# Routing in groups of 16 under a budget of time per step, and first tiles of the second pass prepared within the first

## The chip, the cores and the metric

One core of one Trainium2 chip runs one program. Its engines work side by side, each through its own queue: TensorE (PE, its weight loads shown as PEld), VectorE (DVE), ScalarE (ACT), GpSimd (POOL) and SyncE (SP). SP and POOL issue the DMAs here; POOL's are indirect ones (gathers and scatters by a list of rows). The metric is the device time of one execution in microseconds. The time before is 1279.0 us, the median of 8 runs (1277.34 to 1280.34).

## The reference

x has 16x1024 tokens of 512 numbers. What is computed, cut to what matters (`D` is a number that depends on all of the normalized x):

```python
def reference(x, W_el, b_el, W_le, b_le, router_w, expert_weights):
    xn = layernorm(x)                                   # per token
    # first branch: a filter, and a code word of 24 bits that is corrected
    D = fractal_dimension(xn)
    x1 = ifft(fft(xn) * wave_filter(D, 512)).real
    bits = (sigmoid(x1 @ W_el + b_el) > 0.5)            # 24 per token
    s = x1 + golay_correct(bits) @ W_le + b_le
    # second branch: 8 experts, the best two of each token
    logits = xn @ router_w.T
    probs = softmax(logits)
    topk_vals, topk_idx = top_k(probs, 2)
    topk_w = topk_vals / (topk_vals.sum(-1) + 1e-6)
    expert_out = einsum('nh,eho->eno', xn, expert_weights)
    g = silu(((take(expert_out, topk_idx) + topk_vals) * topk_w).sum())
    return x + s * g
```

## The kernel before

The 16384 tokens are 128 tiles of 128 (`NT`), and the program has two passes. In the first every tile of tokens is filtered, its code word and its two experts are found, and a record of each token (two weights, a bias, mean, scale, token number, corrected bits) is scattered into the list of its pair of experts (28 pairs). In the second pass tokens are gathered by pair, so that all 128 tokens of a tile use the same two expert matrices.

**Pass 1** is the loop of `pass_1` (L1107 to L1190) over g, one tile per step. SP loads x in blocks of four tiles (`load_block`, pool `xin` of 5 buffers, issued `AHEAD_L` = 16 steps ahead) and stores the filtered rows yd in blocks of four. For each tile: DVE folds the rows into sums and differences (`fold`, L445 and L448), ACT takes the sum of squares (`spread`, L459), PE transposes (`transpose`, L528 and L532) and ACT copies the result, PE multiplies by the filter matrix (`filt`, L542), ACT copies yb out (L548), and a step later DVE's `take` (L472) sums the last columns of the product: 8 logits, 24 latent values, and what the mean and scale need.

Around them run many small operations of DVE, kept in lists of closures. `scale` (L477) turns the raw sums of a group of `GT` = 8 tiles into mean and scale, `code` (L560) finds and corrects the bits of such a group, `route` (L631) works on 16 tiles (`RT`): the largest two logits, the pair, the softmax weights, and each token's place in its list, by products with a triangular matrix in PE, a product with a mask (`place`) and a sum (`where`, both of 128x448 numbers). One list each is popped at fixed points of a step: the order below is that of every step, whatever the operations cost.

```python
            routed()
            steps(scales, 1)
            routed()
            steps(now, 1)
            while folds and folds[0][0] <= g:
                fold(*folds.pop(0)[1:])
```

When a round's places are known, POOL scatters one tile's records with each DMA (`lists<-rec,dst`, L791), one or two per step (`throw`). After `SOON` = 80 tiles, `whole_ops` (L861 to L964) finds which full tiles of 128 each pair has by then: POOL gathers their records (`tt`, L915) once the scatters due have been issued, and DVE takes them apart (L926) five steps later. At g = NT-10, NT-4 and NT-1 the first tile of pass 2 is gathered (`lead_x`), normalized and turned. The last group's `scale` is run after the last step.

**Pass 2** (from L1195) has 189 tiles in the order that `kinds` writes out: 28 wholes (`LEAD`), 61 items (tiles of one expert, made of what is left over) mixed with 8 wholes, 5 wholes, and 27 rests (the left-over tokens, whose two products were stored by items) mixed with 60 wholes. I call the stretch of rests and wholes the tail. What is left of routing and the bookkeeping of lists runs within its first steps, and with it the remaining scatters (up to three per step).

Step n of the loop works on products of tile n and on other tiles' earlier and later parts. POOL's queue gets, in this order: `fetch_tok(n+11)` (for items, the entry's gather), `fetch_x(n+8)` (xg, L1082 by way of `gather`), `fetch_parts(n+4)` (two gathers for a rest), `fetch_y` (yg), and `put` of tile n-4 (out, L1433). xg takes a buffer of the pool `xgp` of 14; a tile's result is formed in that same buffer (L1424) and out reads it from there, while an item's buffer is free after `normalize`.

```python
    AHEAD_K, AHEAD_X, AHEAD_P, AHEAD_Y, AHEAD_N, AHEAD_T = 11, 8, 4, 5, 6, 3
    BEHIND = 3
    xgp = ctx.enter_context(tc.tile_pool(name="xgp", bufs=14))
```

DVE gets `normalize(n+6)` (L1267), `triple` (L1339 and L1340: the bits of a tile as b3, 4 steps ahead), `spread_out` and `combine` (L1371 to L1378, L1423, L1424: the first branch joined to the second), and `added` (L1384) or the item's copy (L1395). PE gets the products (L1324; two per whole, one per item, each 8 records), `turn` (L1276) for the first tiles, `turn_code` (L1354) and `mend` (L1366: corrected bits through W_le). ACT gets `scaled` (L1381) and the Silu (L1387), and the halves (L1283) and joins (L1292) around SP's DMA transposes, which replace `turn` from the seventh tile on.

Of the kernel before, what the change touches and what calls it, by code (L numbers as in the profile page):

```python
# [23 lines left out]
ENTRY = META  # L24
IN_RANGE = "worked out on the chip from counts that add up to the number of tokens"
# [9 lines left out]
def kernel(  # L35
# [57 lines left out]
    SOON = 80  # L93
# [24 lines left out]
    xin = p1.enter_context(tc.tile_pool(name="xin", bufs=5))  # L118
# [55 lines left out]
    def loads():  # L174
        nc.sync.dma_start(out=head, in_=xf[0:2, :].rearrange("t (a j) -> (t a) j", j=HW))
        nc.sync.dma_start(out=bas, in_=basis)
        for b in range(2):
            xts[b] = load_block(b, 2 - b)
        nc.scalar.dma_start(out=lat, in_=w_lat)
        nc.scalar.dma_start(out=ident, in_=square[:, 0, :])  # L180
        xts[2] = load_block(2)
        nc.sync.dma_start(out=ht, in_=golay_t)
        nc.sync.dma_start(
            out=row_sb,
            in_=rows.rearrange("(o n) -> o n", o=1).to_broadcast([P, rows.shape[0]]),
        )
        nc.sync.dma_start(out=tri, in_=square[:, 1, :])
        nc.sync.dma_start(out=wl, in_=w_le3)
        nc.sync.dma_start(out=ord_sb, in_=orders)
        for b in range(3, 5):  # L190
            xts[b] = load_block(b)
# [212 lines left out]
    GT = 2 * TPT  # L404
    NG = NT // GT
    AHEAD_L = 16
    RT = 2 * GT
    rounds = [(t, RT) for t in range(0, NT, RT)]

# [6 lines left out]
    recs = [p1c.tile([P, 2 * GT, META], F32, name=f"rec{i}") for i in range(4)]  # L416
# [10 lines left out]
    for s in range(NG):  # L427
        groups[s].rec = recs[(s // 2) % 4][:, (s % 2) * GT : (s % 2 + 1) * GT, :]
# [48 lines left out]
    def scale(s: int):  # L477
# [9 lines left out]
        def off():  # L487
            nc.gpsimd.tensor_copy(k.rec[:, :, MEAN], k.raw[:, :, X])
# [15 lines left out]
        def scaled():  # L504
            if s % 2 == 0:
                k.wide = small.tile([P, 2 * GT, X], F32, name="ex", bufs=2)
                k.ex = k.wide[:, 0:GT]
            else:
                k.ex = groups[s - 1].wide[:, GT:]
# [10 lines left out]
            scaled,  # L520
# [39 lines left out]
    def code(s: int):  # L560
# [64 lines left out]
        turns = [lambda: turn_bits(0), lambda: turn_bits(TPT)]  # L625
        checks = [c0, c1, c2, c3, c4, c5]
        return [bits] + [None] * 5 + turns + [None] * 4 + [syndrome] + [None] * 2 + checks
# [3 lines left out]
    def route(n: int):  # L631
# [6 lines left out]
        def new(name, shape, dt=F32):  # L638
            full = [P, {S: 2 * GT}.get(shape[1], shape[1])] + list(shape[2:])
            made = small.tile(full, dt, name=name, bufs=4 if name == "dst" else 1)  # L640
            return made[:, 0 : shape[1]]
# [7 lines left out]
        def begin():  # L649
            s, j = t0 // GT, t0 % GT  # L650
            st.ex = groups[s].wide[:, j : j + S]
            st.rec = recs[(t0 // (2 * GT)) % 4][:, t0 % (2 * GT) : t0 % (2 * GT) + S, :]
            st.mx = st.m1 = new("mx", [P, S])
            v.tensor_reduce(st.mx, st.ex[:, :, L:X], AX.X, ALU.max)
            v.tensor_copy(st.rec.bitcast(I32)[:, :, TOKEN], tok[:, t0 : t0 + S])

        def shift():
            st.pb = new("pb", SN)
            v.tensor_tensor(st.pb, st.ex[:, :, L:X], wide(st.mx), ALU.subtract)
            nc.scalar.activation(st.pb, st.pb, AF.Exp)  # L660

        def total():
            st.sm = new("sm", [P, S])
            st.den = new("den", [P, S])

            st.ch = small.tile([P, 2, S], F32, name="ch", bufs=1)
            st.wt = small.tile([P, 2, S], F32, name="wt2", bufs=1)
            v.tensor_reduce(st.sm, st.pb, AX.X, ALU.add)


        def largest(src, hot):
            def b():
                st.eq = new("eq", SN)
                v.tensor_tensor(st.eq, src(), wide(st.mx), ALU.is_equal)

            def d():
                st.at = new("at" + hot, [P, S])
                setattr(st, "at" + hot, st.at)
                v.tensor_reduce(st.at, st.eq, AX.X, ALU.max)

            def e():
                setattr(st, hot, new(hot, SN))
                v.tensor_tensor(getattr(st, hot), rv, wide(st.at), ALU.is_equal)

            return [b, lambda: v.tensor_mul(st.eq, st.eq, rv), d, e]

        def rest():
            st.pr = new("pr", SN)
            v.scalar_tensor_tensor(
                st.pr, st.hot1, -1e30, st.ex[:, :, L:X], ALU.mult, ALU.add  # L690
            )

        def second():
            st.mx = new("m", [P, S])
            v.tensor_reduce(st.mx, st.pr, AX.X, ALU.max)

        ops = [begin, shift]
        ops += largest(lambda: st.ex[:, :, L:X], "hot1")
        ops += [rest, second] + largest(lambda: st.pr, "hot2")

        def chosen():

            st.sel = new("sel", [P, S, NE + NE // 2], BF16)
            v.tensor_add(st.sel[:, :, 0:NE], st.hot1, st.hot2)
            v.tensor_copy(st.sel[:, :, NE:], st.sel[:, :, 0 : NE // 2])

        def behind():

            st.p2 = new("p2", [P, S])
            v.tensor_tensor(st.p2, st.mx, st.m1, ALU.subtract)  # L710
            nc.scalar.activation(st.p2, st.p2, AF.Exp)

        ops += [chosen, behind]
        chances = [
            total,
            lambda: v.reciprocal(st.ch[:, 0, :], st.sm),
            lambda: v.tensor_mul(st.ch[:, 1, :], st.p2, st.ch[:, 0, :]),
            lambda: v.scalar_tensor_tensor(  # L718
                st.den, st.ch[:, 0, :], 1e-6, st.ch[:, 1, :], ALU.add, ALU.add
            ),  # L720
            lambda: v.reciprocal(st.den, st.den),
        ]


        def pair(d, at):
            if d == 1:
                st.oh = new("oh", [P, S, NPAIR], BF16)
            n = min(NE, NPAIR - at)
# [4 lines left out]
        for d in range(1, NE // 2 + 1):  # L733
            ops.append(lambda d=d: pair(d, (d - 1) * NE))

        A = S // 4
# [42 lines left out]

        def place():  # L780
            st.pl = new("pl", [P, S, NPAIR])
            v.tensor_mul(st.pl, st.pk, st.oh)

        def where():
            st.dst = new("dst", [P, S], I32)
            with nc.allow_low_precision("whole numbers"):
                v.tensor_reduce(st.dst, st.pl, AX.X, ALU.add)
# [17 lines left out]
        def weigh():  # L805
            v.tensor_mul(st.wt, st.ch, st.den.unsqueeze(1).to_broadcast([P, 2, S]))

        def biases():

            v.tensor_mul(st.ch, st.ch, st.wt)  # L810

        def swap():

            st.lo = new("lo", [P, S])
            v.tensor_tensor(st.lo, st.athot1, st.athot2, ALU.is_gt)
            v.tensor_sub(st.den, st.wt[:, 0, :], st.wt[:, 1, :])

        weights = [
            weigh,
            biases,  # L820
            lambda: v.tensor_add(st.rec[:, :, BIAS], st.ch[:, 0, :], st.ch[:, 1, :]),
            swap,
            lambda: v.tensor_mul(st.lo, st.lo, st.den),
            lambda: v.tensor_add(st.rec[:, :, W0], st.wt[:, 1, :], st.lo),
            lambda: v.tensor_sub(st.rec[:, :, W1], st.wt[:, 0, :], st.lo),
        ]
        ranks = [None, place, where]
# [7 lines left out]
        ops += [quads, runs, None, rank] + chances + weights  # L835
# [244 lines left out]

    def gather(dst, src, idx, limit):
# [25 lines left out]
    def pass_1():  # L1107
        scales = []

        def steps(ops, n):  # L1110
            for _ in range(min(n, len(ops))):
                op = ops.pop(0)
                if op:
                    op()
# [15 lines left out]
        )  # L1130
        loaded = 0
        for g in range(-1, NT):
            if (g + AHEAD_L) % TPT == 0 and 5 <= (g + AHEAD_L) // TPT < NB:
# [14 lines left out]
            if g > 0 and g % GT == 0:  # L1148
                scales += scale(g // GT - 1) + [lambda s=g // GT - 1: now.extend(code(s))]
            for n, (t, size) in enumerate(rounds):  # L1150
                if g == t + size + 4:
                    routes.extend(route(n))
                    if t + size == SOON:
                        routes.append(lambda: whole_ops(0))
            going = True

            def routed():
                nonlocal going
                going = going and bool(routes) and routes[0] is not None
                if going:  # L1160
                    going = routes[0]() is not False
                if going:
                    routes.pop(0)

            routed()
            steps(scales, 1)
            routed()
            steps(now, 1)
            while folds and folds[0][0] <= g:
                fold(*folds.pop(0)[1:])  # L1170
                steps(rest, 1)
            steps(now, 1)
            routed()
            steps(scales, 1)
            routed()
            if going is False and routes and routes[0] is None:
                routes.pop(0)
            steps(now, 1)
            steps(rest, 1)
            if g < NT - TPT:  # L1180
                throw(1 + (g > SOON))
            push(aside)
            if g == NT - 10:
                lead_x()
            if g == NT - 4:
                lead_normal()
        assert loaded == NE * KC
        take(NT - 1)
        for op in scales + scale(NG - 1):
# [495 lines left out]
```

## Time and profile before

| what | value |
|---|---|
| median of 8 runs | 1279.0 us (1277.34 to 1280.34) |
| the profiled execution | 1278.86 us, of it span 1276.9 us |
| mean granted clock of TensorE | 0.984 |
| product L1324, busy | 934.4 us |
| filter L542, busy | 167.5 us |
| POOL: lists L791, out L1433 | 149.1 us (128 DMAs), 111.9 us (100 DMAs) |
| POOL: yg, xg (both L1082) | 111.6 us (101), 108.4 us (100) |
| DVE: folds L445 | 82.7 us |
| pass 1's `take`s | from 16.2 to 290.4 us |
| first product of pass 2 | 300.40 us |
| last out issued | 1268.63 us |

The span is what the profile covers; the 2 us beside it lie before the first and after the last instruction. Busy times of an engine are of its own queue, and those of POOL for a DMA are the time that POOL takes to issue it, not the transfer. In a timeline a line has the start, the duration, the engine and line, and in brackets the idle time of the engine before it and what ended that. The page's own slices show where PE is not full: at the seventh slice (the gather of tt) and at the tenth (the change of pass).

### The profile page before, as it was taken

To read this page: it belongs to the slowest core of one execution; us is meant where nothing else is said; L and a number is where in the kernel's file an instruction comes from. 1 tells how busy PE (TensorE), PEld (TensorE's weight loads), DVE (VectorE), ACT (ScalarE), POOL (GpSimd) and SP (SyncE) were. 2 spreads that over 40 slices of the span, in tenths; PEclk is the share of its full clock that TensorE was granted. 3 is DMA by queue.
4 is the path that set the end of the run, shared out by engine and by line. 5 is a ranking of instruction groups with operands and counts; after the bars stand their busy time and mean duration, and the time that the engine had idled before them with its cause. 6 is when DMAs were issued, how large, how long until landed. Compare 5 with 4: busy or idle time off the path is not lost.

```text
span 1276.9 us, 17149 instructions
## 1 busy us (share of the span) xinstructions
PE 1220.1 (96%) x4417; PEld 679.9 (53%) x4417; DVE 998.4 (78%) x2538; ACT 787.6 (62%) x1326; POOL 799.3 (63%) x764
## 2 busy tenths in 40 slices
PE   9999999697899999999999999999999999999996
PEld 8998888593344444444444444444444444444444
DVE  8899999684877899744444445799999999999996
ACT  7999998494444454565666665465565565555562
POOL 0046665267667475676667633677777777777772
PEclk9999999798899999999999999999999999999998
DMA  8888888545445655889998899788887988878882
GB/s 297 308 296 292 293 289 286 175 159 174 100 114 150 152 158 135 179 223 221 203 213 217 214 209 210 183 200 226 219 214 205 211 221 223 221 211 227 223 212 85
DMA packets 235640, 266.42 MB, mean 209 GB/s; under 512 B 182558, under 2 KB 183070, under 8 KB 227482
## 3 DMA queue, kind: packets, MB, share of 16 engines
q1 hardware_dynamic: 188330, 133.16, 41.7%
q0 software_dynamic: 46928, 132.03, 35.2%
q8 instruction: 40, 0.66, 0.2%
q14 instruction: 54, 0.44, 0.1%
q10 hardware_dynamic: 288, 0.13, 0.0%
HBM read 140.79 MB, written 83.56 MB: 176 GB/s over the span
## 4 chain that ended last, share of the span: by engine, by line
PE 60%; DVE 19%; issue 8%; DMA 6%; POOL 4%; ACT 2%; POOLq 0%; DVEq 0%
PE pe L1324 50%; PE py L542 4%; DVE halved L445 3%; DMA xg<-in_x,toks 2%; DVE yg L1371 2%; DVE acc L1384 2%; PE pt L528 1%; POOL lists L791 1%; POOL out L1433 1%; DVE yg L1423 1%; DVE mix L1374 1%; POOL yg L1082 1%; DVE folded L448 1%; DVE raw L472 1%; DVE xn L1267 1%
## 5 line engine op out<-in xcount | busy, mean ns | idle before, releaser
L1324 PE MATMUL pe<-w_sb,xt 128*128 x2136 | 934.4, 590 | 2.8 <-DVE yg L1371 2.3
L1324 PEld LDWEIGHTS pe<-w_sb,xt 128*128 128x128 f32 x2136 | 403.1, 191 | 455.0 <-issue 431.3
L1292 ACT COPY xt<-plt 128x1024 uint16<-128x1024 uint16 x156 | 209.3, 1342 | 56.7 <-DMA plt<-pl 56.1
L791 POOL DMA_INDIRECT lists<-rec,dst x128 | 149.1, 1165 | 99.6 <-issue 64.6
L1387 ACT ACTIVATE acc<-acc,stats 128x512 f32<-128x512 f32 (+2 forms) x103 | 73.5, 714 | 217.3 <-DVE acc L1384 217.3
L542 PE MATMUL py<-fw,pmt 128*128 128x162 f32 x1024 | 167.5, 306 | 21.5 <-DVE den L718 10.4
L1433 POOL DMA_INDIRECT out<-xg,toks x100 | 111.9, 1119 | 88.6 <-DVE xg L1424 59.6
L1283 ACT COPY pl<-xn 128x1024 uint16<-128x1024 uint16 x156 | 161.9, 1038 | 0.0
L542 PEld LDWEIGHTS py<-fw,pmt 128*128 128x128 f32 x1024 | 146.6, 192 | 27.8 <-ACT yb L548 12.8
L1082 POOL DMA_INDIRECT yg<-yd,toks x101 | 111.6, 1105 | 41.8 <-issue 18.9
L1082 POOL DMA_INDIRECT xg<-in_x,toks x100 | 108.4, 1084 | 42.6 <-issue 29.3
L1384 DVE SCALAR_TENSOR_TENSOR acc<-pe,stats,acc 128x512 f32<-128x512 f32 (+2 forms) x103 | 75.8, 736 | 74.9 <-PE pe L1324 69.3
L1395 DVE COPY part<-pe 128x512 f32<-128x512 f32 x61 | 42.2, 691 | 115.2 <-PE pe L1324 115.1
L1381 ACT ACTIVATE acc<-pe,stats 128x512 f32<-128x512 f32 (+2 forms) x103 | 68.8, 668 | 70.7 <-PE pe L1324 31.5
L548 ACT COPY yb<-py 128x512 f32<-128x512 f32 x128 | 75.4, 589 | 28.0 <-PE py L542 26.1
L459 ACT ACTIVATE no<-xt 128x512 bf16<-128x512 f32 x128 | 92.5, 723 | 0.0
L1424 DVE TENSOR_TENSOR xg<-yg,xg 128x512 f32<-128x512 f32 (+1 forms) x129 | 88.2, 684 | 4.5
L1423 DVE TENSOR_TENSOR yg<-yg,acc 128x512 f32<-128x512 f32 (+1 forms) x130 | 87.9, 676 | 2.4 <-ACT acc L1387 2.4
L1082 POOL DMA_INDIRECT part<-ed,adr_r x54 | 61.7, 1142 | 35.6 <-DVE yg L1371 17.8
L445 DVE TENSOR_TENSOR halved<-xt 128x512 f32<-128x512 f32 (+1 forms) x136 | 82.7, 650 | 0.0
L1082 POOL DMA_INDIRECT entry<-lists,adr_i x61 | 63.6, 1042 | 28.4 <-issue 18.0
L528 PE MATMUL pt<-ident,halved 128*128 128x128 f32 x512 | 78.6, 276 | 0.0
(279 smaller groups left out, 1476.7 us busy)
## 6 DMA issues: line engine op xcount, KB each, us to landing
yd<-yb SPq DMA_DIRECT2D x32, 1024.0 KB
xt<-in_x SPq DMA_DIRECT2D x31, 1024.0 KB
ed<-part SPq DMA_DIRECT2D x61, 256.0 KB
w_sb<-in_expert_w SPq DMA_DIRECT2D x32, 256.0 KB
plt<-pl SPq DMA_TRANSPOSE x156
lists<-rec,dst POOLq DMA_INDIRECT x128
yg<-yd,toks POOLq DMA_INDIRECT x101
xg<-in_x,toks POOLq DMA_INDIRECT x100
```

Of the source, the lines that this page charges most:

```text
L445: op(to[:, :, ::-1] if q else to, x[:, :, a:z], x[:, :, H + a : H + z])
L459: nc.scalar.activation(no, x, AF.Square, bias=x[:, 0:1], scale=-1.0, accum_out=k.sq2[:, j : j + 1],)
L528: nc.tensor.matmul(pt[:, c, :], half, ident, start=(i == 0), stop=(i == 1), is_transpose=True)
L542: nc.tensor.matmul(blocks(py)[:, i // 2, i % 2, :], pmt[:, i, :], fw[:, i, :], start=True, stop=True,)
L791: dma = nc.gpsimd.indirect_dma_start(out=lists, out_offset=bass.IndirectOffsetOnAxis(ap=st.dst[:, j : j + 1], axis=0), in_=st.rec.bitcast( ...
L1082: nc.gpsimd.indirect_dma_start(out=dst, out_offset=None, in_=src, in_offset=bass.IndirectOffsetOnAxis(ap=idx, axis=0), bounds_check=limit - 1,
L1283: nc.scalar.copy(k.pl.rearrange("p (h e) -> p h e", h=2), k.xn.bitcast(U16).rearrange("p (e h) -> p h e", h=2),)
L1292: nc.scalar.copy(k.xt.bitcast(U16).rearrange("p c (t h) -> p h c t", h=2), k.plt.rearrange("p (h c) t -> p h c t", h=2),)
L1324: nc.tensor.matmul(pe[:, o].unsqueeze(1), k.xt[:, c, :], w_sb[:, bass.ds(e, 1), c, o], start=(c == 0), stop=(c == KC - 1),)
L1384: nc.vector.scalar_tensor_tensor(k.acc[:, c], src[:, c], k.w1, k.acc[:, c], ALU.mult, ALU.add)
L1423: nc.vector.tensor_mul(k.mix[:, c], k.mix[:, c], k.acc[:, c])
L1433: dma = nc.gpsimd.indirect_dma_start(out=of, out_offset=bass.IndirectOffsetOnAxis(ap=k.tok, axis=0), in_=k.x, in_offset=None, bounds_check ...
```

## The change

- `GT` becomes 16: `scale` and `code` run once per 16 tiles, on tiles twice as wide, and `route` starts when its round's scale is through. `recs` are four of 16 tiles.
- `route` is written anew. The triangular matrix gets 2^22 (`OWN`) on its diagonal, so a token's place is the largest entry minus OWN (`where`, then `place` on 128x16), in place of a masked product and a sum. The weights follow from other formulas with fewer operations.
- The small operations are no longer popped at fixed points. Each has an estimated cost (`took`; 0.17 us where none is given). A step adds 1.9 us of credit (`STEP`; `LATE`, 2.05, in the last 16 steps), folds and other work use some of it, and `small_ops` goes through the lists while credit is left.
- `AHEAD_L` goes from 16 to 12 and `xin` from 5 to 4 buffers; `SOON` from 80 to 64; the last group's copy of the mean from POOL to ACT; the last group's `scale` into pass 2, after `normalize(1)`.
- b3 of the first four tiles of pass 2 is made in pass 1's last four steps (`triple_of`, `lead.b3`, pool `small` with 5 buffers).
- In pass 2, `turn` is due at k-1, and `turn_code` of the first tiles at k/2, half steps standing between a whole's second product and `added`. `xgp` goes from 14 to 13 buffers.

```diff
-    SOON = 80
+    SOON = 64
...
-    xin = p1.enter_context(tc.tile_pool(name="xin", bufs=5))
+    xin = p1.enter_context(tc.tile_pool(name="xin", bufs=4))
...
-    GT = 2 * TPT
+    GT = 4 * TPT
     NG = NT // GT
-    AHEAD_L = 16
-    RT = 2 * GT
+    AHEAD_L = 12
+    STEP, LATE = 1.9, 2.05
+    RT = GT
...
+    def took(us, op):
+        op.us = us
+        return op
...
-            nc.gpsimd.tensor_copy(k.rec[:, :, MEAN], k.raw[:, :, X])
+            if s < NG - 1:
+                nc.gpsimd.tensor_copy(k.rec[:, :, MEAN], k.raw[:, :, X])
+            else:
+                nc.scalar.copy(k.rec[:, :, MEAN], k.raw[:, :, X])
...
+        def where():
+            st.far = new("far", [P, S])
+            v.tensor_reduce(st.far, st.pk, AX.X, ALU.max)
+
         def place():
-            st.pl = new("pl", [P, S, NPAIR])
-            v.tensor_mul(st.pl, st.pk, st.oh)
-
-        def where():
             st.dst = new("dst", [P, S], I32)
             with nc.allow_low_precision("whole numbers"):
-                v.tensor_reduce(st.dst, st.pl, AX.X, ALU.add)
+                v.tensor_scalar(st.dst, st.far, -OWN, None, ALU.add)
...
+        def small_ops(n):
+            nonlocal credit
+            for _ in range(n):
+                going = False
+                for ops in (scales, routes, now):
+                    if credit <= 0 or not ops or ops[0] is None or id(ops) in waiting:
+                        continue
+                    if ops[0]() is False:
+                        waiting.add(id(ops))
+                        continue
+                    credit -= getattr(ops.pop(0), "us", 0.17)
+                    going = True
+                if not going:
+                    break
...
+            credit = min(credit, 0.4) + (STEP if g < NT - 16 else LATE) - 0.21
+            waiting.clear()
+            small_ops(1)
             while folds and folds[0][0] <= g:
-                fold(*folds.pop(0)[1:])
+                b, i, js = folds.pop(0)[1:]
+                fold(b, i, js)
+                credit -= 1.2 * (js.stop - js.start) / TPT
                 steps(rest, 1)
...
+            small_ops(99)
...
+            if g >= NT - 4:
+                n = len(lead.b3)
+                lead.b3.append(triple_of(masks[0][:, n : n + 1]))
         assert loaded == NE * KC
         take(NT - 1)
-        for op in scales + scale(NG - 1):
+        for op in scales:
             op()
...
-    xgp = ctx.enter_context(tc.tile_pool(name="xgp", bufs=14))
+    xgp = ctx.enter_context(tc.tile_pool(name="xgp", bufs=13))
...
+        k.b3 = lead.b3.pop(0) if lead.b3 else triple_of(k.bits)
...
-            added(k, product(k, expert(k, 1)))
+            pe = product(k, expert(k, 1))
+            those(k.at - 0.5, "turn_code", turn_code)
+            added(k, pe)
...
         "turn": [
-            None if crossed[k] else max(k - AHEAD_T, min(k - 2, 3)) for k in range(NTILE)
+            None if crossed[k] else k - 1 for k in range(NTILE)
         ],
...
-        "turn_code": [k - 3 for k in range(NTILE)],
+        "turn_code": [max(k / 2, k - 3) for k in range(NTILE)],
...
             each(n + AHEAD_N, normalize)
+            if n + AHEAD_N == 1:
+                for op in scale(NG - 1):
+                    op()
```

## The prediction, made before the changed kernel was run

> **What bounds the kernel now.** I read the page's busy shares first, then windows by stage, then POOL's waits, then its timeline where it looks full.
>
> ```profile
> PE 1220.1 (96%) x4417; PEld 679.9 (53%) x4417; DVE 998.4 (78%) x2538; ACT 787.6 (62%) x1326; POOL 799.3 (63%) x764
> ```
>
> TensorE is busy 96% of the span, so only about 57 us can come from its gaps. By stage (columns: length, then PE, PEld, DVE, ACT and POOL busy, PE clock, DMA share, GB/s):
>
> ```profile
> 129.70:162.72 33.02, 30.64 (x238) 29.13 (x239) 30.41 (x107) 30.02 (x77) 20.06 (x18) 1.00 0.88 298
> 291.00:345.00 54.00, 41.38 (x110) 19.43 (x111) 33.49 (x104) 20.60 (x35) 39.09 (x39) 0.81 0.49 142
> 345.00:500.00 155.00, 155.00 (x409) 69.94 (x408) 130.30 (x300) 77.10 (x105) 100.08 (x91) 1.00 0.57 144
> 790.00:1230.00 440.00, 436.66 (x1130) 196.08 (x1129) 408.59 (x904) 252.10 (x373) 335.24 (x299) 1.00 0.83 213
> ```
>
> The first row is one round of 16 tiles of pass 1: PE, DVE and ACT are all near 30 of 33 us. The second is the change of pass, with 12.6 us of PE idle and a clock of 0.81. In the third and fourth PE has no holes. POOL's 335 of 440 us in the last row looks like slack, but it is not. That is seen in what its idle time is waiting for (total, times, longest), in 790 to 1230:
>
> ```profile
> POOL xg L1082 <- issue: 24.3, 78, 0.7
> POOL out L1433 <- issue: 23.8, 78, 0.3
> POOL xg L1082 <- DMA out<-xg,toks: 4.6, 3, 2.0
> ```
>
> Nearly every POOL instruction of the tail (tiles that need an out, from about 796) starts 0.3 us after the previous one: it runs back to back, and the 0.3 us is issue, not waiting. From 796 to 1230 it holds 296 DMAs, 331.8 us busy and, at 0.30 each, about 90 us of issue: 422 of 434 us. About 12 us is true slack. A rest and two wholes issue 11 of them (3 xg, 3 yg, 3 out, 2 part), some 15.3 us against 15.5 us of TensorE work. So POOL is second to PE by 1%, and the xg gathers, 25 us or more ahead of their normalize at 811, are only 3.4 to 5 us ahead after 1020.
>
> **The change, part by part.** The sum starts from the profiled execution, 1278.86 us (span 1276.9), which is the median of the runs, 1279.0, to 0.01%.
>
> *VectorE's routing in pass 1.* Per 16 tiles the small operations were about 70 (two scales, two codes and one route) with 17.2 us of durations, and become about 51 with 13.6: the second scale and code go, and the route's 42 become about 37. I priced the new ones by the same shapes (128x16 at 0.17, 128x128 at 0.27, 128x448 at 0.6). Durations overlap; starts lie some 0.085 us closer:
>
> ```profile
> 283.30 0.18 DVE L821 TENSOR_TENSOR rec<-ch 128x16 f32<-128x16 f32 x1
> 283.38 0.17 DVE L815 TENSOR_TENSOR lo<-athot,athot 128x16 f32<-128x16 f32 x1
> 283.47 0.17 DVE L816 TENSOR_TENSOR den<-wt 128x16 f32<-128x16 f32 x1
> ```
>
> So the time is 17.2 - 70x0.085 = 11.25, and after 13.6 - 51x0.085 = 9.25: 2.0 us per round. PE-bound steps of 1.76 us (filters at 132.50, 134.26, 136.02) set the floor: 16x1.76 and about 2.0 of side matmuls is 30.2 against 33.02, so 2.0 fits below it. Over 7 rounds: **-14**. The budget (1.9 us a step, 2.05 in the last 16) spreads the operations but holds only about 12.6 us of small operations a round by the kernel's own prices, whose sum is 12.7; if it falls behind, the routing piles up at the end: +2.4. If all rounds reach the floor, 7x2.8 = -20.
>
> *The stall at the first whole_ops* (SOON 80 to 64). POOL's gather of the lists waits 5.36 us for the last scatter, and VectorE's copy of it at 243.92 waits 9.95 us for that; both stand in the step order 5 steps apart, as before. About 12 us is lost there with a clock of 0.50 after it; it comes earlier, not shorter: 0, plus or minus 5.
>
> *Blocks of x* (5 to 4 buffers, issued 12 steps ahead). First use is 7 steps, some 13 us, after the issue, where a load takes 7 to 9 us behind SP's stores, and VectorE's fold of xt has 0.0 us of idle before it: 0, hidden by those 13 us, and 1 to 2 us a block if that cover went. The last mean copy on ACT (0.2 us) and scale(NG-1) within pass 2 are covered by the change of pass.
>
> *The change of pass.* The first product waits for `triple`, `turn` and turn_code, which queue on VectorE behind a normalize that waits for its gather:
>
> ```profile
> 298.02 0.31 PE L1354 MATMUL pc<-ident_b,b 128*96 128x128 bf16 x1 [8.65 <-DVE b L1340]
> 300.40 5.54 PE L1324 MATMUL pe<-w_sb,xt 128*128 x8 [0.27 <-issue]
> ```
>
> Pass 1's last matmul ends at 289.38. With four b3 made in pass 1 and turn_code later, the first product can start near 290.7. What is late next is turn(1): its normalize has its gather at 294.2, so the second starts at about 295.6 instead of 306.27, 10.7 us earlier. Later gaps (a 3.5 us one before 325.51, for spread_out behind routing) remain, and the routing of the last round still stands in this stage. I take **-10**, between 0 (the gap only moves to them) and -17 (all but the clock recovered).
>
> *xgp from 14 to 13 buffers.* This is a wait added to POOL's queue. At step n POOL issues xg for tile n+8 and then out for tile n-4. With 14 buffers xg takes the buffer of tile n-6, whose out is the last but one on POOL; with 13 that of tile n-5, whose out is the instruction issued just before it (a yg or a part rarely lies between). The trace shows the old wait:
>
> ```profile
> 1003.61 1.10 POOL L1433 DMA_INDIRECT out<-xg,toks  x1 [0.30 <-issue]
> 1005.02 1.07 POOL L1082 DMA_INDIRECT xg<-in_x,toks  x1 [0.31 <-issue]
> 1006.39 1.01 POOL L1082 DMA_INDIRECT yg<-yd,toks  x1 [0.30 <-DVE b L1340]
> 1007.71 1.15 POOL L1433 DMA_INDIRECT out<-xg,toks  x1 [0.30 <-issue]
> 1010.23 1.02 POOL L1082 DMA_INDIRECT xg<-in_x,toks  x1 [1.37 <-DMA out<-xg,toks]
> ```
>
> The gather at 1010.23 waited for the out of 1003.61, landed 6.6 us after its start, not for that of 1007.71. Four such waits in the tail give landings of 5.7 to 7.6 us; the other 76 gathers start about 5.4 us after that out and do not wait, so most land sooner. After the change the distance is on average 1.53 us over the 80 gathers from 800 on, and whatever the landing exceeds this POOL stands still, with yg, out, part and the next xg queued behind. PE has no reserve to cover it: the 25 us lead goes once, and goes already now.
>
> The landing time L has no row of its own. The floor is the last out, alone on the queues; its bytes move until about 1270.8, 2.2 us after its start:
>
> ```profile
> 1268.63 0.97 POOL L1433 DMA_INDIRECT out<-xg,toks  x1 [3.16 <-DVE xg L1424]
> ...
> 1270.20:1270.60 0.40, 0.00 (x0) 0.00 (x0) 0.00 (x0) 0.00 (x0) 0.00 (x0) 0.50 0.99 379
> 1270.60:1271.00 0.40, 0.00 (x0) 0.00 (x0) 0.00 (x0) 0.00 (x0) 0.00 (x0) 0.50 0.57 215
> ```
>
> The nearest row under load is a gather of the same 256 KB with VectorE standing and waiting for it: nine have 3.41 to 4.88 us, median 3.6, as here:
>
> ```profile
> 1073.68 1.14 POOL L1082 DMA_INDIRECT xg<-in_x,toks  x1 [0.31 <-issue]
> ...
> 1077.09 0.55 DVE L1267 TENSOR_SCALAR xn<-xg,stats 128x512 f32<-128x512 f32 x1 [0.84 <-DMA xg<-in_x,toks]
> ```
>
> Summing (L - distance) over the 80 gathers gives 55 us at 2.2, 118 at 3.0, 166 at 3.6, 238 at 4.5, 302 at 5.3. The 12 us of slack comes off. I take 3.6: **+154**; ends +43 and +290. In the first 28 wholes scatters lie between out and xg, or POOL has time (4.2 us of DMAs and 2 of wait against 7 per tile), and the items free their buffers at normalize, so there it costs 0.
>
> The Trainium skill ("DMA: Bandwidth & Descriptors", Anatomy of one DMA — SWDGE (gpsimd) path) fits one such DMA at 2.0 us plus its bytes over 436 GB/s, mostly the write's receipt. For 256 KB that is an estimate of 2.6 us, below the loaded rows here; with it the tail term would be near 75 and the total near 1330.
>
> *Sum:* 1278.9 - 14 - 10 + 154 = **1409 us**.
>
> **Rivals.**
> - *The window wait does not bind* (other side). If an out frees its buffer within about 1.8 us of its start, as the back-to-back POOL row would let one hope, only the savings are left: 1278.9 - 24 = 1255. The waits of 5.7 to 7.6 us and the floor of 2.2 speak against it; for it, I saw no out's release directly at this distance. Chance 0.12.
> - *Lands at the floor.* As POOL slows, the DMA share of 0.83 falls and L sinks to 2.2 to 2.5: 1278.9 - 24 + 43 = 1298. Against it, the loaded rows are at least 3.4. Chance 0.15.
> - *Heavier.* L nearer the visible waits, 5.3: 1278.9 - 24 + 290 = 1545; PE's new gaps of some 2 us per product could also halve its clock, as the gap of 3.5 us before 325.51 was followed by 0.50. At half clock throughout, a cycle's 15.5 us of PE becomes 31, against 21.5 for POOL: another 9.5x27 = 256, an upper bound. Chance 0.13. The skill ("TensorE: Matmul & The Clock Gate", HAM oscillation) sets the limit at gaps over about 3.4 us, which agrees with the 3.5; by it 2 us gaps would leave the clock whole.
> - *It does not do what it says:* savings and wait both near nothing. Chance 0.02.
>
> **How the numbers follow.** The forecast has 0.58, with its own range 1345 to 1490 (L from 3.0, 1361, to 4.5, 1481, with the ends of the other terms). The overall range reaches down to the floor case and up into the heavier one, 1290 to 1500; the 1255 case (0.12) and the larger part of the heavier one (0.08) stay outside. A measurement of this kernel tells about 0.2%, 2.6 us, from no change. Faster is the first rival alone, 0.12; same 0.02; slower 0.86.
>
> **What would show it.** Right: in the tail, xg gathers wait for DMA out some 2 us each, 160 us in all; PE falls to about 70% busy there; pass 1's rounds take about 31 us; the first product follows pass 1's last matmul by 1 to 2 us. Wrong, if xg's waits for out stay at a few us in all, if xg and the out before it belong to buffers farther apart than I count, or if the budget leaves routing for the end of pass 1.

## The result, and the profile after

The changed kernel takes 1446.6 us (median of 16 runs, 1437.4 to 1460.7), the kernel before 1279.7 us in the same comparison: a ratio of 1.1303, 95% interval [1.1286, 1.1321]. The profiled execution after took 1450.4 us, of it span 1448.4. Medians are of all executions and ratios of those in the usual, faster state, so the two need not divide out exactly. The last two sets of experiments below ran on two other chips, where the kernel before itself takes 1419 and 1420 us; there only ratios to it are compared.

Below are the page's busy shares after, and from its 40 slices the rows of TensorE and of its clock. From the 24th slice on PE is no longer full:

```profile
PE 1278.5 (88%) x4417; PEld 691.2 (48%) x4417; DVE 984.0 (68%) x2386; ACT 779.0 (54%) x1301; POOL 783.4 (54%) x755
...
PE   9999989879999999999999977778778787878777
PEclk9999989999999999999999999898889899888999
```

The same by stage: the steps of pass 1, the change of pass, the first wholes, the items, the tail (columns as before: length, then PE, PEld, DVE, ACT, POOL busy, PE clock, DMA share, GB/s):

```profile
12.00:272.00 260.00, 247.66 (x1905) 236.15 (x1903) 227.38 (x699) 233.50 (x574) 112.09 (x100) 0.98 0.81 281
272.00:320.00 48.00, 35.04 (x99) 15.83 (x100) 30.33 (x88) 17.30 (x36) 37.17 (x36) 0.93 0.54 151
320.00:480.00 160.00, 160.00 (x428) 72.61 (x427) 132.86 (x302) 79.02 (x108) 101.10 (x93) 1.00 0.58 136
480.00:767.00 287.00, 287.00 (x684) 127.06 (x683) 136.32 (x269) 173.09 (x175) 184.65 (x179) 1.00 0.90 211
767.00:1400.00 633.00, 502.83 (x1133) 211.14 (x1132) 413.21 (x905) 253.05 (x374) 323.12 (x297) 0.89 0.58 149
```

Everything up to 767 runs earlier than before, and the 440 us of the prediction's row for the tail have become 633, with no more POOL work in them (323 us, 335 before). The 101st gather of xg, just ahead of the tail, stands at 741.13 (761.82 before), 20.7 us earlier; the span ends 171.5 us later. So the tail alone lost 192.2 us. POOL's waits in 900 to 1400 (total, times, longest) say where:

```profile
POOL xg L1100 <- DMA out<-xg,toks: 126.9, 45, 5.1
POOL xg L1100 <- DMA out<-xg,rentry: 59.4, 19, 4.8
POOL out L1457 <- issue: 20.1, 66, 0.3
```

64 gathers of xg stand 186.3 us for an out. No POOL instruction there waits for a result of an engine longer than the usual issue of 0.3 us, so POOL, with these waits in its queue, is what sets the pace. Its timeline shows which out it is:

```profile
1106.29 1.34 POOL L1100 DMA_INDIRECT yg<-yd,toks  x1 [0.30 <-DVE yg L1447]
1107.94 1.06 POOL L1457 DMA_INDIRECT out<-xg,rentry  x1 [0.30 <-issue]
1111.19 1.23 POOL L1100 DMA_INDIRECT xg<-in_x,rentry  x1 [2.19 <-DMA out<-xg,rentry]
1112.72 1.01 POOL L1100 DMA_INDIRECT yg<-yd,rentry  x1 [0.30 <-issue]
1114.04 1.03 POOL L1457 DMA_INDIRECT out<-xg,toks  x1 [0.30 <-issue]
1117.38 1.02 POOL L1100 DMA_INDIRECT xg<-in_x,toks  x1 [2.31 <-DMA out<-xg,toks]
```

Each xg waits for the out right in front of it. Over the 79 gathers from 740 on that wait so, the time from the start of that out to the start of xg is 3.14 us at the least, 3.99 in the middle of the list and 4.06 in the mean.

In pass 1 the rounds of 16 tiles, from `take` to `take`, read as follows (the last row holds the gather of tt):

```profile
76.70:106.90 30.20, 30.07 (x240) 29.03 (x239) 28.48 (x88) 29.26 (x75) 20.50 (x19) 1.00 0.91 314
106.90:138.30 31.40, 30.48 (x241) 29.05 (x240) 28.33 (x90) 29.46 (x75) 20.91 (x18) 1.00 0.90 313
138.30:169.80 31.50, 30.33 (x240) 28.91 (x239) 28.57 (x89) 29.23 (x74) 19.40 (x18) 1.00 0.88 304
169.80:214.60 44.80, 37.41 (x258) 34.31 (x258) 31.29 (x96) 30.09 (x74) 17.06 (x17) 0.89 0.73 245
```

Three rounds of 30.2 to 31.5 us stand where there were three of 33.0, with VectorE at 28.5 instead of 30.4 us of busy time: 1.9 less. PE, at 30.1 to 30.5, is now next to the whole of a round.

### The profile page after: what moved, and what is told of

It reads as the page before. It is cut to its first block, busy times and chain, and to the rows that moved or that the text cites. A ratio compares the mean times of both kernels' runs of the same rounds, so it can differ in the third digit from the quotient of the medians.

```text
span 1448.4 us, 16975 instructions
## 1 busy us (share of the span) xinstructions
PE 1278.5 (88%) x4417; PEld 691.2 (48%) x4417; DVE 984.0 (68%) x2386; ACT 779.0 (54%) x1301; POOL 783.4 (54%) x755
## 4 chain that ended last, share of the span: by engine, by line
PE 43%; issue 20%; DVE 12%; POOL 12%; DMA 7%; ACT 4%; POOLq 0%; DVEq 0%; ACTq 0%
PE pe L1354 35%; POOL out L1457 5%; POOL yg L1100 4%; DMA xg<-in_x,toks 4%; PE py L546 4%; DVE halved L450 2%; POOL part L1100 2%; DMA out<-xg,toks 2%; ACT yb L552 1%; PE pt L532 1%; DVE yg L1393 1%; ACT pmt L538 1%; POOL xg L1100 1%; ACT no L464 1%; DVE xn L1297 1%
## 5 line engine op out<-in xcount | busy, mean ns | idle before, releaser
L1354 PE MATMUL pe<-w_sb,xt 128*128 x2136 | 977.7, 612 | 8.2 <-DVE yg L1393 2.7
L1354 PEld LDWEIGHTS pe<-w_sb,xt 128*128 128x128 f32 x2136 | 416.6, 199 | 511.8 <-issue 480.3
L1297 DVE TENSOR_SCALAR xn<-xg,stats 128x512 f32<-128x512 f32 x100 | 55.7, 559 | 213.0 <-DMA xg<-in_x,toks 205.8
L811 POOL DMA_INDIRECT lists<-rec,dst x128 | 146.2, 1142 | 98.7 <-issue 48.8
L1376 PEld LDWEIGHTS <-b 128*96 128x96 bf16 x128 | 16.1, 126 | 167.5 <-DVE b L1089 149.0
```

Source lines behind the costliest of these rows:

```text
L811: dma = nc.gpsimd.indirect_dma_start(out=lists, out_offset=bass.IndirectOffsetOnAxis(ap=st.dst[:, j : j + 1], axis=0), in_=st.rec.bitcast( ...
L1354: nc.tensor.matmul(pe[:, o].unsqueeze(1), k.xt[:, c, :], w_sb[:, bass.ds(e, 1), c, o], start=(c == 0), stop=(c == KC - 1),)
```

## The experiments

**Is it the buffer?** Three kernels, the first with xgp back at 14 (ct gives up two buffers to make room in SBUF):

```diff
-    xgp = ctx.enter_context(tc.tile_pool(name="xgp", bufs=13))
+    xgp = ctx.enter_context(tc.tile_pool(name="xgp", bufs=14))
...
-        k.ct = w2.tile([96, P], BF16, name="ct", bufs=6)
+        k.ct = w2.tile([96, P], BF16, name="ct", bufs=4)
```

> The changed kernel with xgp back at 14 buffers; to make room for it the pool of ct has 4 buffers instead of 6. Theory (the wait of xg for the out issued just before it costs the whole loss): that wait goes, xg waits for the last out but one as before, and what the change saves before the tail is left, about 21 us by the xg gathers up to the tail (1259), so 1250 to 1265. Rival (something else of the change, in the new routing or the turns, slows the tail, and the waits only show it): 1400 or more. Second rival (both): in between, near 1350.

Measured: 1260.4 us beside 1281.3 of before, 0.9831 [0.9776, 0.9886]. Its waits of POOL in 790 to 1230:

```profile
POOL xg L1100 <- issue: 21.5, 70, 0.4
...
POOL xg L1100 <- DMA out<-xg,toks: 9.9, 7, 2.5
```

Nearly all gathers follow at the 0.3 us of issue again, and all of the loss is gone. The second kernel is the kernel before with 13:

```diff
-    xgp = ctx.enter_context(tc.tile_pool(name="xgp", bufs=14))
+    xgp = ctx.enter_context(tc.tile_pool(name="xgp", bufs=13))
```

> The kernel before with xgp at 13 and nothing else. Theory: the tail's 190 us come alone and the savings don't: 1455 to 1485, with some 78 gathers of xg waiting about 2.7 us each for the out in front of them. Rival (the rest of the change does it): 1275 to 1290.

Measured: 1472.1 us, 1.1485 [1.141, 1.1559], which is 190.7 us over before. In 790 to 1400:

```profile
POOL xg L1082 <- DMA out<-xg,toks: 155.9, 54, 5.6
POOL xg L1082 <- DMA out<-xg,rentry: 68.2, 22, 4.6
```

One number changed in the old kernel brings the same wait (mean distance 4.03 us over 80 gathers) and the same loss. The two parts add up: -21.0 (a14) and +190.7 (b13) are 169.7, where the whole change is 166.9. The third keeps 13 buffers and asks for one tile less ahead:

```diff
-    AHEAD_K, AHEAD_X, AHEAD_P, AHEAD_Y, AHEAD_N, AHEAD_T = 11, 8, 4, 5, 6, 3
+    AHEAD_K, AHEAD_X, AHEAD_P, AHEAD_Y, AHEAD_N, AHEAD_T = 11, 7, 4, 5, 6, 3
```

> The changed kernel with 13 buffers, but xg issued for tile n+7 instead of n+8, so that it takes the buffer of tile n-6, whose out is the last but one. Theory: the distance to that out is that of the kernel before, and the loss goes: 1255 to 1275 (the upper end if normalize, one step after the gather, waits for it). Rival (fewer buffers cost by themselves, whatever the distance): 1400 or more.

Measured: 1273.6 us, 0.9947 [0.9919, 0.9974]. So 13 buffers by themselves cost at most the 13 us by which this kernel is behind a14, and not the 186; it is the distance between the out and the gather that needs its buffer. In the two profiled executions ax7 is 7.6 us behind, all of it from the second half of the tail. What lengthens it was not tested; a likely part is the normalize, which has the gather one step later, and in 790 to 1400 waits 20.8 us for it, where a14 waits 10.7:

```profile
DVE xn L1297 <- DMA xg<-in_x,toks: 20.8, 12, 3.7
```

**Does the price follow the distance?** The same instructions, with xg last of the step's gathers:

```diff
-            each(n + AHEAD_X, fetch_x)
             each(n + AHEAD_P, fetch_parts)
             those(n, "fetch_y", fetch_y)
+            each(n + AHEAD_X, fetch_x)
```

> The changed kernel with POOL's order within a step turned: part and yg before xg, so that a yg (1.3 us with its issue) lies between an out and the xg that waits for it, and for a rest two parts more. Theory (each xg waits until about 4.07 us after the start of that out): 87 x 1.3 = 114 us less, and some 20 to 35 for the parts: 1295 to 1340. Rival (the tail is slow for another reason, and the wait is only where POOL stands): 1430 to 1450.

Measured: 1314.4 us in one run, 132 less than the changed kernel, within the expected band. The timeline shows the yg between the two, and a wait that is shorter by it:

```profile
1106.02 1.03 POOL L1457 DMA_INDIRECT out<-xg,toks  x1 [0.30 <-issue]
1107.36 1.03 POOL L1100 DMA_INDIRECT yg<-yd,toks  x1 [0.31 <-issue]
1109.96 1.01 POOL L1100 DMA_INDIRECT xg<-in_x,toks  x1 [1.57 <-DMA out<-xg,toks]
```

The out lands about as late as before (3.94 us here); what is put between is time that POOL doesn't lose. Nothing but POOL's order changed, and in this one run some 70% of the loss (132 of 186 us) went.

**What the savings are made of.** Four kernels with a14 as their base ran on a second chip, on which the kernel before took 1419.2 us; then a14 itself and three of them once more (the names with _again) ran on a third, on which it took 1420.4. `turns_old` undoes the preparation of pass 2:

```diff
-            if g >= NT - 4:
-                n = len(lead.b3)
-                lead.b3.append(triple_of(masks[0][:, n : n + 1]))
...
-            None if crossed[k] else k - 1 for k in range(NTILE)
+            None if crossed[k] else max(k - AHEAD_T, min(k - 2, 3)) for k in range(NTILE)
...
-        "turn_code": [max(k / 2, k - 3) for k in range(NTILE)],
+        "turn_code": [k - 3 for k in range(NTILE)],
```

> The changed kernel with 14 buffers of xgp (a14, 1260.4), and of its preparation of pass 2 the b3 made in pass 1, the turn at k-1 and the turn_code at k/2 undone. Theory (the early first product is mostly given back by waits that follow it, as the products by then are only 4 to 5 us nearer): 1264 to 1267, with the first product near 284. Rival (the preparation is worth the 10 us of the forecast or more): 1270 or more.

> As turns_old, beside a14 on one chip. Theory (the early first product is mostly given back): 3 to 7 us more than a14. Rival (the preparation is worth the forecast's 10 us or more): 10 us or more.

`no_budget` lets the small operations go as they come:

```diff
-    STEP, LATE = 1.9, 2.05
+    STEP, LATE = 99.0, 99.0
```

> a14 with 99 us of credit per step, so that small operations are held back by nothing but their own gaps. Theory (fewer operations make pass 1 shorter; when they run within the round matters less): 1257 to 1265. Rival (the budget itself matters: without it VectorE works off operations that wait for PE and ACT, with take and fold queued behind them): 1275 or more.

> As no_budget, beside a14 on one chip. The rounds before the disturbance of the first attempt took 40.1 and 43.5 us, where a14 has 31.8 and 29.3. Theory now (without the budget VectorE stands in operations that wait for PE and ACT): 10 us a round over 7 rounds, 1310 to 1350. Rival (that was the disturbance; only the number of operations matters): 1257 to 1270.

`soon80` moves the first whole_ops back, and `apart12` gives the gather of tt seven steps more:

```diff
-    SOON = 64
+    SOON = 80
```

> a14 with SOON at 80 again. Theory (the stall at the gather of tt is the same and only stands elsewhere): 1258 to 1263. Rival (its place, or the number of scatters that are left for pass 2, matters): more than 3 us either way.

```diff
-        aside.extend([experts, None, fetch] + [None] * 5 + [apart, None, None, turned, None, kept])
+        aside.extend([experts, None, fetch] + [None] * (5 if part else 12) + [apart, None, None, turned, None, kept])
```

> a14 with 12 steps instead of 5 between the first gather of tt and VectorE's copy of it; the second whole_ops is left as it is. Theory (the copy waits for a gather that needs some 8 us to land and is itself held for the last scatter; the round with it is 13 us longer than its neighbours): the round comes down to some 31 to 33 us, 1248 to 1252. Rival (the round is long because of whole_ops' own work on VectorE and PE): 1257 to 1261.

> As apart12, beside a14 on one chip. Theory (the round with the stall is 13 us long because VectorE's copy waits for the gather of tt): 8 to 13 us less than a14, and that round near 32 us. Rival (whole_ops' own work makes it long): within 3 us of a14.

> a14 once more, as the measure for the three kernels beside it: 1257 to 1264, with the kernel before at 1277 to 1284.

Measured, as ratios to the kernel before on the same chip:

| kernel | median us | ratio, 95% interval |
|---|---|---|
| a14_again | 1438.7 | 1.0028 [0.9972, 1.0084] |
| turns_old | 1436.3 | 1.0218 [1.0108, 1.0329] |
| turns_old_again | 1431.4 | 1.006 [1.0021, 1.01] |
| no_budget | 1446.5 | 1.0252 [1.0153, 1.0351] |
| no_budget_again | 1460.5 | 1.0185 [1.009, 1.0279] |
| soon80 | 1404.2 | 0.994 [0.9884, 0.9996] |
| apart12 | 1439.4 | no interval |
| apart12_again | 1436.7 | 1.006 [1.0012, 1.0108] |

All absolute expectations are missed, because the measure itself moved by 140 us. Where the time goes is visible, if not why: TensorE, VectorE and ScalarE stand together, and DMA with them, every now and then. The first two rounds of a14_again take 31.8 and 29.3 us, as a14's do; the third takes 44.1 in place of 30.2. The first such place in soon80:

```profile
80.00:90.00 10.00, 8.75 (x67) 8.18 (x66) 7.72 (x22) 7.24 (x20) 8.00 (x8) 1.00 0.89 305
90.00:100.00 10.00, 3.17 (x23) 2.55 (x21) 4.11 (x14) 4.02 (x12) 7.57 (x8) 0.98 0.23 79
```

PE, at 8.75 of 10 us, falls to 3.17, VectorE from 7.72 to 4.11, and DMA from 0.89 to 0.23, while POOL goes on. With that, differences of 3 to 13 us can't be told: what the preparation of pass 2, SOON and the distance of tt's copy are worth was not settled by taking them away. The first four have no a14 beside them on their chip, and of the three that have, the intervals of turns_old_again and apart12_again overlap a14_again's. Nor did a14's gain show on the third chip; it stands for the first alone. For the budget there is a little more. The interval of no_budget_again lies wholly above that of a14_again beside it, by a hair, and the first round, which in a14_again is free of the disturbance, takes 40.1 us in both runs without the budget, and 31.8 in a14 on the first chip and in a14_again on the third. First no_budget, then a14, in the round from take 1 to take 17:

```profile
16.00:56.10 40.10, 32.85 (x239) 30.63 (x238) 35.43 (x105) 30.98 (x73) 0.24 (x1) 0.89 0.70 253
```

```profile
15.70:47.50 31.80, 30.84 (x238) 29.77 (x237) 28.00 (x72) 29.98 (x70) 0.24 (x1) 1.00 0.82 291
```

Without the budget 105 instead of 72 VectorE instructions fall into it, so part of the 8.3 us is routing drawn forward. But PE, which has its product of the routing in the same queue as the filters, stands for it (no_budget_again, in that round):

```profile
PE pg L777 <- DVE oh L709: 6.4, 1, 6.4
```

In a14 PE waits 0.6 us in all from 16 to 100. So holding operations back is worth something; how much, of the 17 us that pass 1 became shorter, stays open.

## Why the prediction was right

The forecast was 1409 us, the result 1446.6, inside the likeliest case's own range. The savings of the other parts came to 22.0 us up to the tail where 24 had been forecast, by two errors in opposite directions (below): that they nearly cancel is luck. By its steps:

- **xgp, the deciding step: mechanism right, size short.** It took L, the landing of an out after its start, as 3.6 us, from gathers of the same size for which VectorE stood. Measured, it is 4.06 in the mean. With the prediction's own sums (166 at 3.6, 238 at 4.5, so 80 for each us) that gives 166 + 0.46x80 - 12 = 191, and the tail lost 192.2, closer than a slack that was itself only estimated at 12 lets one expect. The row chosen was a gather seen by its reader, in place of an out seen by its successor. The floor of 2.2 us, from the bytes of an out alone on the queues, was lower than any of the 79 waits (3.14). By the trace's packet records both parts of the time are longer than that: the last packet of POOL's queue ends 3.1 us after the start of the out (the middle of the list; 2.5 at the least; 2.4 by the same records for the last out of the kernel before, alone), and xg starts another 0.6 us later, of which 0.3 is its issue. In the first wholes, where the prediction put the cost at 0, 14 gathers wait for an out as well, 32 us in all, and cost nothing: the products are 22.0 us ahead of the kernel before from the 129th record to the 1201st.
- **The Trainium skill's fit** ("DMA: Bandwidth & Descriptors", Anatomy of one DMA — SWDGE (gpsimd) path), which the prediction put at an estimated 2.6 us for 256 KB, is below every distance measured here. The trace decides for this case: about 4 us, at a DMA share of 0.58.
- **VectorE's routing, -14:** the last `take` of pass 1 moved from 290.36 to 272.74, -17.6. Of this, 3 us is the stall at the gather of tt, which the prediction called "not shorter" and left at 0 within 5: VectorE's copy waits 4.93 us in place of 9.95, and the round with it is 13 us over its neighbours instead of 16.5. The other 14.6 is the size of the term, and 2.0 us per round of VectorE was 1.9; that it is VectorE's shorter work and not the budget was not separated.

```profile
202.34 1.28 DVE L930 COPY ttf<-tt 30x640 f32<-30x640 f32 x1 [4.93 <-DMA tt<-lists,idx]
```

- **The change of pass, -10: too much.** The first product came 27.3 us earlier (273.09), the second 25.7, but from the 129th record of the products on only 22.0 is left (374.19 to 352.16): 17.6 from pass 1 and 4.4 from here. The trace names the takers: the second product's turn waits for a normalize that waits for its gather, as forecast, and then come spread_out and the last round's routing, which now stand behind it.

```profile
280.02 0.66 PE L1306 MATMUL pt<-ident,xn 128*128 128x128 f32 x4 [3.23 <-DVE xn L1297]
...
303.44 3.70 PE L1354 MATMUL pe<-w_sb,xt 128*128 x8 [2.70 <-DVE yg L1393]
...
311.52 0.35 PE L777 MATMUL pg<-oh,tri_b 128*128 128x448 bf16 x1 [4.21 <-ACT bt L583]
```

  That the preparation is worth 4.4 us is read from this trace alone; the kernel without it gave no answer.
- **The rival "does not bind"** (1255) was what the kernel would have been with its wait taken away: a14 measured 1260.4. Its condition, a release within 1.8 us, was met by none of the 79. The rival "lands at the floor", in which L falls with the DMA share, fell too: the share went from 0.83 to 0.58, and L was 4.06 and not 2.2 to 2.5.
- **What would show it:** "some 2 us each, 160 in all" was 235 us over 79 gathers from 740 to the end, issue included; "PE about 70% busy" was 79%. PE is busier than forecast because it is slower: its clock in the tail is 0.89, and what was 474 us of PE work before (789 to the end) is 539 after (767 to the end). At the old 474 the share would have been 70%. The waits bunch, and after a gap of 3.78 us four records of a product take 3.02 us:

```profile
1269.00 3.60 PE L1354 MATMUL pe<-w_sb,xt 128*128 x8
1276.37 0.26 PE L1376 MATMUL pc<-ident_b,b 128*96 128x128 bf16 x1 [3.78 <-DVE b L1089]
1277.03 0.38 PE L1388 MATMUL pg<-wle,ct 96*128 96x512 bf16 x1 [0.40 <-DVE yg L1393]
1277.24 3.02 PE L1354 MATMUL pe<-w_sb,xt 128*128 x4
```

  I had left the half clock to the heavier rival. It came, and cost nothing that shows: POOL does not wait for VectorE or PE in that stretch, and the loss is accounted for by L alone. The limit in length of a gap that the prediction set beside it does not hold in this case. The gap before 325.51, which it read as 3.5 us, is 2.32 in the trace, with a matmul of 0.38 and 0.81 of idle time in front of it, and the clock was down to 0.81 on average already from 324 to 325. In the tail after (780 to 1405) PE has 25 gaps of 2.4 us and more; a clock of 0.50 follows within 4 us on 24 of them, among them seven of the eight from 2.4 to 3.0 us, and not on the one of 1.81.

## What to carry to other kernels

A pool's number of buffers is a distance in a queue: count which instruction frees the buffer that the next one takes, and how far in front it stands on the same queue. Here one buffer less moved that release from some four DMAs back to the instruction just in front, and on POOL, which ran back to back, the landing time less that distance was then paid with every tile. Before a buffer is given up, see whether asking for the tile one step later, or putting another transfer between, keeps the distance; and where SBUF is short by a few hundred bytes, look for them in a pool whose buffers nobody waits for, as two of ct's six here.

## What the runs showed of the hardware that I had not expected

- An indirect write of 256 KB to HBM let the gather that waited for its buffer start 3.14 us after its own start at the earliest and 4.0 as a rule, at a DMA share of 0.58. Its packets take 3.1 us of that, where those of the last out of the kernel before, alone on the queues, took 2.4.
- TensorE's clock fell to half after gaps of only 2.4 us: 24 of the 25 gaps from there on in the tail were followed by 0.50, the one of 1.81 us was not.
- The same kernel took 1419 and 1420 us on two other chips, 11% more. The kernels traced there have stretches in which TensorE, VectorE, ScalarE and DMA stand together; in the one shown PE is idle for 6.8 of 10 us, and VectorE's longest wait in it, 4.2 us, is put down to "issue". A gain of 1.7% on the first chip was not to be seen on the one where it was tried (1.0028 [0.9972, 1.0084]). What causes it stays open.
